# A four-layer graph network: single-head f1 rows and a fourth adjacency buffer in the decoder, later pair additions, a moved bias row, and a merged weight product cut in two

## The chip, the cores and the metric

The kernel runs on one core of a Trainium2 chip. The metric is the device time of one execution in microseconds (us), as the median of several runs. Beside the runs there is one profiled execution, from which every view of the profile comes.

## The reference

Everything is float32. There are 2708 nodes with 512 features, and one dense adjacency matrix of zeros and ones (about 1.2% ones, ones on the diagonal). Four layers follow each other, each with a residual and a layer norm: x = layernorm(x + layer(x, adj)).

Layer 0 is an attention encoder, an MLP, and a decoder that uses the same attention again. The adjacency is given to it twice (as "local" and as "long range" pattern), so that both halves of `att` are the same. It has 4 heads of 128 features:

```
Xw  = per head  x @ W                       f1, f2 = Xw . V[:,0], Xw . V[:,1]
att = softmax over j of sigmoid(f1[i] + f2[j]), where adj[i, j] is not 0
Xn  = batchnorm(att @ Xw)
emb = batchnorm(elu(Xn @ enc_W.T + b) + Xn)
Y   = elu(per head (att @ emb) @ W.T)
out = batchnorm(elu(Y @ dec_W.T + b) + Y)
```

Layer 1 is A @ (x W + b) with each row divided by the node's degree. Layer 2 is a masked softmax attention with scores (x E)(x E).T. Layer 3 is a softmax attention with query, key and value weights, to whose scores the adjacency is added twice:

```
attn = softmax((x Wq + bq) @ (x Wk + bk).T / sqrt(512) + adj + adj);   out = attn @ (x Wv + bv)
```

## The kernel before, in words

Nodes are cut into 22 blocks of 128 (the last has 20). The whole of layer 0 works on transposed tiles: rows of a tile are the neighbours j of one block, its columns the nodes i of one half (`HSPAN`: two halves of 1354). The four heads go in two pairs (`HP` = 2). An attention pass (`attention_pass`) has therefore four passes, (half, pair) = (0,0), (0,1), (1,0), (1,1), of 22 blocks each, in the order `ORDER`; a block's index in that order is its *place*. The function runs twice: as the encoder (`first` true) and as the decoder.

For each block `form` makes the tile `t` of both heads (128 x 2708): it loads the adjacency block `a` (677 KB) on the SP queue (L369), ScalarE takes a tanh of the row f1 plus the block's f2 for each head (L396), VectorE multiplies by the adjacency (L404, which turns what is not linked into a large negative number), and ScalarE takes the exponential of both heads (L405). TensorE then multiplies it into six accumulators `po` (L471). There are four buffers of `t`, and of `a` four in the encoder and three in the decoder. The rows f1, broadcast to all partitions, come as one tile `f1b` of both heads in two buffers (L423). Five of the 22 tiles of each pass are written to memory by the encoder (`KEPT`) and read back by the decoder instead of being formed. In the passes of the first pair the encoder also prepares the adjacency itself: VectorE makes a mask `z` (L385, a tag with one buffer), adds it (L386), and POOL writes the block to `adj_d` (L390), from which the later passes read. In the decoder VectorE also counts the zeros of each block for layer 1 (`count`, L346).

In the encoder TensorE also adds up the columns of each tile (`psm`, L494). In the passes of the second pair, places 4 to 19 are first added in pairs on VectorE (L488), in place in the first tile of the pair, so that TensorE sums one tile for two.

At the end of an encoder pass `keep` copies the accumulators into `ft` (L580), and after pass (0,1) it makes the product of the MLP's weights with the batch norm's beta (L585: `small_product`, whose result goes through one row, here a tile with the tag "z"). Sums go through memory (`sum_d`, `few`, `rs_d`, `rb`) and their reciprocals scale `ft` in steps that are taken up between the places of the next pass.

Between encoder and decoder wq and wk are transposed into `wqT` and `wkT`, the MLP's weights are scaled by the batch norm (L684, L688), the query and key weights of layer 3 are merged into one 512 x 512 matrix `mqk` (L696, four row blocks of four matmuls; L705 writes it to `mqk_d`), and the MLP runs over six chunks of columns (L724), with a second small product for the mean (L733). At the end of a decoder pass `take` moves the accumulators out (L825); after the last one comes the decoder's MLP (L859, `ps_dec`), whose statistics give the last batch norm. The hidden rows of layer 1 follow at once (`tp_out` L996, `ps_hid` L128 by L998); before them VectorE clears a part of `hid_hi` (L966) and copies the weights into `w_sb` (L976).

The order of the instructions on each engine is laid out when the kernel is compiled, by a scheduler that takes readiness into account; each engine then works in that order. A buffer of a pool is reused when the last reader of its former tile is done, and a pool that opens in the room of a closed one waits for the last users of that room, transfers included. `tc.issue_after(x)` keeps an instruction behind x.

The lines that hold the f1 rows and the pair additions:

```
f1b = att.tile([P, HP, HW], F32, tag="f1b", name="f1b", bufs=2)
...
whole, m = before, P
nc.vector.tensor_tensor(whole[:n, :, :w], whole[:n, :, :w], tv, ALU.add)
```

Of the kernel before, what the change touches and what calls it, by code (L numbers as in the profile page):

```python
# [1 line left out]

# [6 lines left out]
F32 = mybir.dt.float32  # L9
# [3 lines left out]
AF = mybir.ActivationFunctionType  # L13
ALU = mybir.AluOpType
# [3 lines left out]
P = 128  # L18
# [11 lines left out]
def gnn_stack_kernel(  # L30
# [25 lines left out]
    nc = tc.nc  # L56
    N, F = x.shape
    H = w0.shape[1]
    C = F // P
# [103 lines left out]
    dram = ctx.enter_context(tc.tile_pool(name="dram", bufs=1, space=bass.MemoryType.DRAM))  # L163
    adj_d = dram.tile([N, N], F32, name="adj_d")
    mqk_d = dram.tile([C, P, C, P], F32, name="mqk_d")
    qscale = float(1.0 / F**0.5)
    uq = const.tile([P, C], F32, name="uq")

# [2 lines left out]
    with ExitStack() as l0:  # L171
# [40 lines left out]
        def project(att, psum):  # L212
# [97 lines left out]
                    copies(f2h[:, NT - 1, :])  # L310
                    nc.vector.tensor_scalar(bm1, prm_sb[:, MB_DEC, :], 1.0, None, ALU.subtract)

            return f1b, blocks, spread, rest

        def spread_sums(att, hf, p):

# [15 lines left out]
        def attention_pass(values, first, att, psum, finish, f1b=None, blocks=(), spread=None, rest=None, taken={}):  # L332
# [5 lines left out]
            def count(hf, jt, att, a=None):  # L338

                h0, w = HSPAN[hf]  # L340
                j0, n = BLOCKS[jt]
                if a is None:
                    a = att.tile([P, HW], F32, tag="a", name="a", bufs=3)
                    nc.sync.dma_start(a[:n, :w], adj_d[j0 : j0 + n, h0 : h0 + w])
                z = att.tile([P, HW], U8, tag="z", name="z", bufs=1)
                nc.vector.tensor_scalar(  # L346
                    z[:n, :w],
                    a[:n, :w],
                    -0.5 * BIG,
                    None,  # L350
                    ALU.is_lt,
                    ALU.add,
                    accum_out=zeros[:n, jt, hf : hf + 1],
                )

            def form(hf, p, jt, att, prepare, f1b, tv):
# [4 lines left out]
                if prepare and hf == 0 and jt < len(blocks):  # L361
                    a = blocks[jt]
                else:
                    a = att.tile([P, HW], F32, tag="a", name="a", bufs=4 if first else 3)

                    early = prepare and hf == 0 and jt < len(blocks) + 2
                    with tc.issue_after(spread.ins) if early else nullcontext():
                        loads.append(
                            nc.sync.dma_start(a[:n, :w], src[j0 : j0 + n, h0 : h0 + w])  # L369
                        )  # L370
# [23 lines left out]
                for k in range(HP):  # L394
                    h = HP * p + k
                    nc.scalar.activation(  # L396
                        tv[:, k, :],
                        f1b[:n, k, :w],
                        AF.Tanh,
                        bias=f2h[:n, jt, h : h + 1],  # L400
                        scale=0.5,
                    )
# [13 lines left out]
            for hf, (h0, w) in enumerate(HSPAN):  # L416
                for p in range(H // HP):
                    prepare = first and p == 0
                    if f1b is None or not prepare or hf > 0:
                        f1b = att.tile([P, HP, HW], F32, tag="f1b", name="f1b", bufs=2)  # L420

                        with tc.issue_after(loads[-9].ins) if len(loads) > 8 else nullcontext():
                            nc.sync.dma_start(  # L423
                                f1b[:, :, :w],
                                f1_d[HP * p : HP * (p + 1), h0 : h0 + w].partition_broadcast(P),
                            )
                    rb = None if first else spread_sums(att, hf, p)
                    sums = None
                    if first and rest is None:
                        sums = sum_tiles()  # L430
                    before = None
                    for place, jt in enumerate(ORDER):
                        n = BLOCKS[jt][1]

# [24 lines left out]
                        if po is None:  # L459


                            both = [
                                psum.tile([P, HP, BANK], F32, tag=f"po{q}", name="po", bufs=1)
                                for q in range(HB)
                            ]
                            po = [both[q][:, k, :] for k in range(HP) for q in range(HB)]
                        for k in range(HP):
                            h = HP * p + k
                            for q, (q0, qw) in enumerate(HCH[hf]):
                                r = 0 if n == P else q * Q  # L470
                                nc.tensor.matmul(  # L471
                                    po[HB * k + q][:, :qw],
                                    values[r : r + n, jt, h * P : (h + 1) * P],
                                    t[r : r + n, k, q0 : q0 + qw],
                                    start=(place == 0),
                                    stop=(place == NT - 1),
                                )
                        if not first:
                            continue

                        if prepare or not ALONE <= place < NT - LAST:
                            whole, m = t, n
                        elif place % 2 == 0:
                            before = t
                            continue
                        else:
                            whole, m = before, P
                            nc.vector.tensor_tensor(  # L488
                                whole[:n, :, :w], whole[:n, :, :w], tv, ALU.add
                            )  # L490
                        for k in range(HP):
                            for r, (q0, qw) in enumerate(SCH[hf]):

                                nc.tensor.matmul(  # L494
                                    sums[k][32 * r : 32 * r + 32, :SW],
                                    ones32[:m],
                                    whole[:m, k, q0 + qw - SW : q0 + qw],
                                    start=(place == 0),
                                    stop=(place == NT - 1),
                                )  # L500
                    later += finish(hf, p, po, sums if first else rb) or []
            for work in later:
                work()
# [59 lines left out]
        with (  # L563
# [8 lines left out]
            def keep(hf, p, po, sums):  # L572
# [4 lines left out]
                for k in range(HP):  # L577
                    for q, (q0, qw) in enumerate(HCH[hf]):
# [1 line left out]
                        taken[q % 2] = copy(  # L580
                            ft[:, HP * p + k, h0 + q0 : h0 + q0 + qw], po[HB * k + q][:, :qw]
                        )
                if hf == 0 and p == 1:
                    row = att.tile([P, HW], F32, tag="z", name="row", bufs=1)[:1, :F]
                    ps = small_product(po[0], mlp_w[0], prm_sb[:, B_ENC, :], row)  # L585
                    nc.vector.tensor_tensor(bias[:, 0, :], ps, prm_sb[:, MB_ENC, :], ALU.add)
                sm = [att.tile([P, BW], F32, tag="rs", name="sm") for _ in range(HP)]
                if not final:
                    for k in range(HP):
# [50 lines left out]

            attention_pass(xw, True, att, psum, keep, f1b, blocks, spread, rest, taken)
            scale1, mean1 = batch_scale(stats, G_ENC, "bn1")


            emb = rows_tile("emb")
# [28 lines left out]
        with (  # L674
            tc.tile_pool(name="att_c", bufs=1) as att,
            tc.tile_pool(name="ps_c", bufs=1, space=PSUM) as psum,
        ):

            (enc_w,) = mlp_w
            for c in range(C):
                if c % 2:
                    nc.scalar.activation(  # L684
# [4 lines left out]
                        enc_w[:, c, :], enc_w[:, c, :], scale1[:, c : c + 1], None, ALU.mult  # L689
                    )  # L690
            stats = stats_tile("stats_b", NCH)
            mqk = emb[:, NT - 3 * C : NT - 2 * C, :]
            for c in range(C):
                ps = psum.tile([P, F], F32, tag="misc", name="ps_m", bufs=2)
                for o in range(C):
                    nc.tensor.matmul(  # L696
                        ps,
                        wqT[:, o, c * P : (c + 1) * P],
                        wkT[:, o, :],
                        start=(o == 0),  # L700
                        stop=(o == C - 1),
                    )
                nc.scalar.activation(mqk[:, c, :], ps, AF.Copy, scale=qscale)
            for o in range(C):
                nc.gpsimd.dma_start(mqk_d[o], mqk[:, :, o * P : (o + 1) * P])  # L705

            row = emb[:1, NT - 3 * C - 2 : NT - 3 * C, :]
            pu = small_product(
                psum.tile([P, F], F32, tag="misc", name="ps_u", bufs=2),
                wkT,  # L710
# [5 lines left out]
            for ci, (c0, w) in enumerate(CHUNKS):  # L716
                pss = []
                for o in range(C):
# [10 lines left out]
                            stop=(c == C - 1),  # L729
                        )  # L730
                    pss.append(ps)
                    if ci == 0 and o == 0:
                        pm = small_product(  # L733
                            psum.tile([P, F], F32, tag="misc", name="ps_mean", bufs=2),
                            enc_w,
                            mean1,
                            row[:, 1, :],
                        )
                        nc.vector.tensor_tensor(bias[:, 0, :], bias[:, 0, :], pm, ALU.subtract)
                        nc.vector.tensor_scalar(  # L740
                            bias[:, 1, :], bias[:, 0, :], 1.0, None, ALU.subtract
                        )
                for o in range(C):
                    dst = ft[:, o, c0 : c0 + w]
                    r = elu(
# [22 lines left out]
            dec_w = load_mlp(dec_wT, "dec_w")  # L768
            links = {}
            spare = []  # L770

            def centre(pm):

# [33 lines left out]
            def decode(hf, p, po, rb):  # L807
# [45 lines left out]
                def mlp(q, o, st, wide):  # L853
# [2 lines left out]
                    q0, qw = HCH[hf][q]  # L856
                    ps = psum.tile([P, BANK], F32, tag="misc", name="ps_dec", bufs=2)
                    for c in range(C):
                        nc.tensor.matmul(  # L859
                            ps[:, :qw],  # L860
                            dec_w[:, c, o * P : (o + 1) * P],
                            t[:, c, q0 : q0 + qw],
# [70 lines left out]
                for q in range(HB):  # L933
# [8 lines left out]
                    if q == 0:  # L942
                        centre(po[0])
                    mlp(q, 3, st, True)

            attention_pass(emb, False, att, psum, decode)
        dsum = small.tile([P, NT], F32, tag="dsum", name="dsum")
# [811 lines left out]
```

## Time and profile before

| what | value |
|---|---|
| median of 3 runs | 3288.74 us (3287.61 to 3291.08) |
| the profiled execution's own time | 3290.97 us |
| its span in the profile | 3289.2 us |
| mean granted TensorE clock | 0.991 |
| TensorE busy | 3221.7 us (98%) |
| VectorE, ScalarE busy | 1944.6 us (59%), 1348.5 us (41%) |
| encoder attention | about 45 to 574 us |
| weights, encoder MLP | about 574 to 703 us |
| decoder attention, its MLP | about 703 to 1202 us |
| layer 1 | about 1209 to 1515 us |
| layers 2 and 3 | about 1515 to 3289 us |

How to read the views: PE is TensorE (PEld its weight loads), DVE VectorE, ACT ScalarE, POOL GpSimd, SP the engine that issues most transfers. L471 is line 471 of the kernel before. A float32 matmul appears as two passes, so that 12 passes are six matmuls. A row of the timeline has start, length, engine, line, operation, what is written and read, and the number of instructions merged; the bracket at its end is the idle time of that engine before it, with the instruction that ended it. A row of the busy times by stretch has the stretch, its length, the busy time of PE, PEld, DVE, ACT and POOL with counts of instructions, the granted TensorE clock as a share of full speed, the busy share of the transfer engines, and GB/s.

### The profile page before, as it was taken

The page shows a single profiled execution, that of the slowest core. Times are in us where ns is not written, and L with a number is a line of the kernel's source. Part 1 is how long each engine was busy: PE and PEld are TensorE (multiplying, and loading weights), DVE is VectorE, ACT ScalarE, POOL GpSimd, SP SyncE. Part 2 cuts the span into 40 slices and gives each one's busy share as a digit, 9 for nine tenths or more (in the row PEclk, how much of TensorE's full clock was granted, in tenths as well). Part 3 has the DMA queues.
Part 4 walks back from the last instruction along what each step waited for, and adds up shares of the span by engine and source line. Part 5 has one row for each costly group of instructions (what it writes and reads, how often), then busy time and mean ns, then how long its engine had stood idle before and what let it go on. Part 6 is the DMA issues. An engine that isn't in the chain of part 4 may idle for free.

```text
span 3289.2 us, 30359 instructions
## 1 busy us (share of the span) xinstructions
PE 3221.7 (98%) x10922; PEld 1722.4 (52%) x10922; DVE 1944.6 (59%) x3144; ACT 1348.5 (41%) x1512; POOL 129.7 (4%) x211
## 2 busy tenths in 40 slices
PE   8998999999999999999999999999999999999999
PEld 5443444454444445885555555554455555555554
DVE  7877977767687596445136666777252452543433
ACT  6887887557877753001133434443020120210211
POOL 1100100000000000000011000000000000000000
PEclk9999999999999999999999999999999999999999
DMA  8855863335555322550034444554211111111100
GB/s 283 305 187 171 302 233 124 106 102 183 185 179 172 134 81 67 144 145 21 0 102 133 122 124 136 148 159 125 68 49 33 44 31 43 40 34 43 36 24 20
DMA packets 172550, 381.45 MB, mean 116 GB/s; under 512 B 20938, under 2 KB 115094, under 8 KB 167982
## 3 DMA queue, kind: packets, MB, share of 16 engines
q1 hardware_dynamic: 156926, 308.16, 30.9%
q0 software_dynamic: 15472, 71.33, 5.8%
q8 instruction: 86, 1.41, 0.2%
q14 instruction: 66, 0.54, 0.1%
HBM read 307.22 MB, written 71.67 MB: 115 GB/s over the span
## 4 chain that ended last, share of the span: by engine, by line
PE 88%; DVE 5%; ACT 2%; DMA 2%; issue 1%; SPq 0%; DVEq 0%; ACTq 0%
PE po L1324 23%; PE po L471 19%; PE ps_s L1203 18%; PE ps_nb L1056 6%; PE ps_wide L1105 4%; PE psm L494 3%; DVE t L404 2%; PE ps_hid L128 2%; PE ps_sup L1501 2%; PE ps_o L1432 2%; PE ps_mlp L724 2%; PE ps_dec L859 2%; DMA a<-adj_d 1%; ACT t L405 1%; ACT t L396 1%
## 5 line engine op out<-in xcount | busy, mean ns | idle before, releaser
L404 DVE SCALAR_TENSOR_TENSOR t<-t,a 128x2708 f32<-128x2708 f32 (+1 forms) x156 | 462.2, 2975 | 124.1 <-ACT t L396 120.1
L396 ACT ACTIVATE t<-f1b,f2h 128x1354 f32<-128x1354 f32 (+1 forms) x312 | 428.3, 1413 | 60.5 <-PE po L471 28.7
L471 PE MATMUL po<-t,xw 128*128 128x452 f32 (+3 forms) x1056 | 415.9, 557 | 14.6 <-ACT t L405 14.6
L405 ACT ACTIVATE t<-t 128x2708 f32<-128x2708 f32 (+1 forms) x156 | 382.6, 2455 | 112.7 <-DVE t L404 112.4
L471 PE MATMUL po<-t,emb 128*128 128x452 f32 (+3 forms) x1056 | 403.1, 550 | 12.3 <-ACT t L405 9.2
L1203 PE MATMUL ps_s<-sup,hT 128*128 128x384 f32 (+1 forms) x1176 | 407.4, 490 | 0.0
L1324 PE MATMUL po<-sup,e 128*128 128x512 f32 x882 | 407.0, 595 | 0.0
L1324 PE MATMUL po<-e,xs 128*128 128x384 f32 (+1 forms) x1176 | 406.0, 489 | 0.0
L1635 DVE SCALAR_TENSOR_TENSOR e<-a_cols,ps_s 128x384 f32<-128x384 f32 (+1 forms) x154 | 85.5, 556 | 451.1 <-PE ps_s L1203 428.2
L471 PEld LDWEIGHTS po<-t,xw 128*128 128x128 f32 (+1 forms) x1056 | 191.5, 193 | 227.4 <-issue 202.0
L1203 PEld LDWEIGHTS ps_s<-sup,hT 128*128 128x128 f32 x1176 | 221.8, 190 | 164.2 <-issue 14.2
L471 PEld LDWEIGHTS po<-t,emb 128*128 128x128 f32 (+1 forms) x1056 | 194.9, 192 | 213.5 <-issue 188.7
L1324 PEld LDWEIGHTS po<-e,xs 128*128 128x128 f32 x1176 | 222.2, 190 | 160.2 <-issue 5.8
L1324 PEld LDWEIGHTS po<-sup,e 128*128 128x128 f32 x882 | 160.4, 190 | 159.3 <-issue 137.1
L1203 PE MATMUL ps_s<-hT 128*128 128x384 f32 (+5 forms) x672 | 211.1, 461 | 0.9 <-ACT sup L1508 0.7
L1302 ACT ACTIVATE e<-e 128x384 f32<-128x384 f32 (+1 forms) x308 | 151.7, 522 | 116.0 <-DVE e L1301 113.3
L1056 PE MATMUL ps_nb<-hid_hi,at 128*128 128x512 f32 x484 | 185.4, 390 | 0.4 <-DVE at L1048 0.4
L1550 ACT ACTIVATE a_cols<-a_cols,neg_big 128x384 f32<-128x384 f32 (+1 forms) x154 | 94.7, 617 | 220.9 <-DMA a_cols<-in_adjT_dram 183.3
L1056 PE MATMUL ps_nb<-hid_lo,at 128*128 128x512 f32 x462 | 179.9, 389 | 0.0
L108 ACT ACTIVATE ln_rstd<-ln_rstd 128x1 f32<-128x1 f32 (+1 forms) x88 | 17.2, 201 | 391.7 <-DVE ln_rstd L107 391.2
L1301 DVE TENSOR_TENSOR e<-e,nmax 128x384 f32<-128x384 f32 (+1 forms) x308 | 163.1, 552 | 23.3 <-ACT nmax L1294 23.3
L1203 PEld LDWEIGHTS ps_s<-hT 128*128 128x128 f32 x672 | 123.1, 190 | 89.5 <-issue 19.4
(252 smaller groups left out, 3325.8 us busy)
## 6 DMA issues: line engine op xcount, KB each, us to landing
a<-adj_d SPq DMA_DIRECT2D x110, 677.0 KB
a_cols<-in_adjT_dram SPq DMA_DIRECT2D x378, 192.0 KB
a<-in_adjT_dram SPq DMA_DIRECT2D x42, 677.0 KB
adj_d<-a POOLq DMA_DIRECT2D x42, 677.0 KB, 5.5
raw<-in_adjT_dram SPq DMA_DIRECT2D x105, 256.0 KB
kept<-t POOLq DMA_DIRECT2D x16, 1354.0 KB, 6.8
t<-kept SPq DMA_DIRECT2D x16, 1354.0 KB
a_cols<-in_adjT_dram SPq DMA_DIRECT2D x63, 202.0 KB
```

The source lines that it names most:

```text
L396: nc.scalar.activation(tv[:, k, :], f1b[:n, k, :w], AF.Tanh, bias=f2h[:n, jt, h : h + 1], scale=0.5,)
L404: step = nc.vector.scalar_tensor_tensor(tv, tv, GUARD, ab, ALU.add, ALU.mult)
L405: nc.scalar.activation(tv, tv, AF.Exp, scale=0.5)
L471: nc.tensor.matmul(po[HB * k + q][:, :qw], values[r : r + n, jt, h * P : (h + 1) * P], t[r : r + n, k, q0 : q0 + qw], start=(place == 0), ...
L494: nc.tensor.matmul(sums[k][32 * r : 32 * r + 32, :SW], ones32[:m], whole[:m, k, q0 + qw - SW : q0 + qw], start=(place == 0), stop=(place = ...
L1056: nc.tensor.matmul(pos[it][:n], at, half[:, jt, :], start=(jt == 0 and k == 0), stop=(jt == NT - 1),)
L1105: nc.tensor.matmul(ps[:, :width], w(c, o), xt(c), start=(c == 0), stop=(c == C - 1),)
L1203: nc.tensor.matmul(ps[:, b * P : w], keys[:, c, j0 : j0 + P], st["q"][:, c, b * P :], start=(c == 0), stop=(c == C - 1),)
L1301: nc.vector.tensor_tensor(e, e, st["nmax"][:, :w], ALU.add)
L1302: nc.scalar.activation(e, e, AF.Exp)
L1324: nc.tensor.matmul(out, lhsT, rhs, start=(k == 0), stop=(k == NT - 1))
L1550: nc.scalar.activation(a, a, AF.Identity, bias=neg_big[: a.shape[0]], scale=1.0e30)
```

## The change

1. *Decoder, f1 rows.* In the decoder the row of each head is a tile of its own, in three buffers. The first head's row is loaded on the SP queue, the second head's on POOL's. The encoder keeps the tile of both heads.
2. *Decoder, adjacency.* `a` has four buffers there too.
3. *Encoder, pair additions.* The addition of a pair of tiles, and its column sums, are taken up at the next place: the addition is kept behind the next tile's multiplication by the adjacency, and the sums stand ahead of that tile's matmuls.
4. *Bias of the encoder's MLP.* The product with beta after pass (0,1) and the product with the mean are gone; one product with the shift (beta - mean x scale) is made from the unscaled weights, before they are scaled and before the MLP.
5. *Merged weights.* Two of the four row blocks of `mqk` stay where they were. `wkT` and half of `wqT` are written to memory from POOL, read back on SP into two `t` buffers at the end of the decoder, and the other two row blocks are made there, behind the last matmul of the decoder's MLP; ScalarE copies them out and POOL writes them to `mqk_d`.

The diff, cut to its core:

```
+    wqT_d = dram.tile([P, C, C // 2 * P], F32, name="wqT_d")
+    wkT_d = dram.tile([P, C, F], F32, name="wkT_d")
...
-                    a = att.tile([P, HW], F32, tag="a", name="a", bufs=4 if first else 3)
+                    a = att.tile([P, HW], F32, tag="a", name="a", bufs=4)
...
+                        else:
+                            f1b = [
+                                att.tile([P, HW], F32, tag="f1b", name="f1b", bufs=HP + 1)
+                                for k in range(HP)
+                            ]
+                            with early:
+                                nc.sync.dma_start(f1b[0][:, :w], f1[:, 0, :])
+                            nc.gpsimd.dma_start(f1b[1][:, :w], f1[:, 1, :])
...
+                        if waiting is not None:
+                            waiting(step)
+                            waiting = None
                         for k in range(HP):
...
+                        def add_up(whole, m, more, first_one, last_one, behind=None):
+                            if more is not None:
+                                with tc.issue_after(behind.ins):
+                                    nc.vector.tensor_tensor(
+                                        whole[: more.shape[0], :, :w],
+                                        whole[: more.shape[0], :, :w],
+                                        more,
+                                        ALU.add,
+                                    )
+                            for k in range(HP):
+                                for r, (q0, qw) in enumerate(SCH[hf]):
+                                    nc.tensor.matmul(
...
+                        if single:
+                            add_up(t, n, None, place == 0, place == NT - 1)
                         else:
+                            waiting = partial(add_up, before, P, tv, False, False)
...
-                if hf == 0 and p == 1:
-                    row = att.tile([P, HW], F32, tag="z", name="row", bufs=1)[:1, :F]
-                    ps = small_product(po[0], mlp_w[0], prm_sb[:, B_ENC, :], row)
-                    nc.vector.tensor_tensor(bias[:, 0, :], ps, prm_sb[:, MB_ENC, :], ALU.add)
...
+            shift1 = batch_shift(scale1, mean1, B_ENC, "bn1")
...
+            merged(0)
+            (enc_w,) = mlp_w
+            row = emb[:1, NT - 3 * C - 2 : NT - 3 * C, :]
+            pm = small_product(
+                psum.tile([P, F], F32, tag="misc", name="ps_shift", bufs=2),
+                enc_w,
+                shift1,
+                row[:, 1, :],
+            )
...
+            nc.gpsimd.dma_start(wkT_d, wkT)
+            nc.gpsimd.dma_start(wqT_d, wqT[:, :, half * P :])
+            merged(1)
             for o in range(C):
-                nc.gpsimd.dma_start(mqk_d[o], mqk[:, :, o * P : (o + 1) * P])
+                nc.gpsimd.dma_start(
+                    mqk_d[o][:, :half, :], mqk[:, :half, o * P : (o + 1) * P]
+                )
...
-                    if ci == 0 and o == 0:
-                        pm = small_product(
-                            psum.tile([P, F], F32, tag="misc", name="ps_mean", bufs=2),
...
+                nc.sync.dma_start(wk_again, wkT_d)
+                nc.sync.dma_start(wq_again, wqT_d)
+                with tc.issue_after(last_dec[0].ins):
+                    for c in range(half):
+                        for o in range(C):
+                            nc.tensor.matmul(
+                                po[1 + c],
+                                wq_again[:, o, c * P : (c + 1) * P],
+                                wk_again[:, o, :],
+                                start=(o == 0),
+                                stop=(o == C - 1),
+                            )
+                for c in range(half):
+                    nc.scalar.activation(mqk[:, c, :], po[1 + c], AF.Copy, scale=qscale)
+                    nc.gpsimd.dma_start(
+                        mqk_d[:, :, half + c, :].rearrange("o p i -> p o i"),
+                        mqk[:, c, :].rearrange("p (o i) -> p o i", o=C),
+                    )
```

## The prediction

> **What bounds the kernel now.** I read the page first: is one engine the bound, and does its clock hold?
>
> ```profile
> PE 3221.7 (98%) x10922; PEld 1722.4 (52%) x10922; DVE 1944.6 (59%) x3144; ACT 1348.5 (41%) x1512; POOL 129.7 (4%) x211
> PEclk9999999999999999999999999999999999999999
> ```
>
> TensorE is busy for 98% of the span. Only two things can pay: TensorE work taken away, and TensorE gaps. So next I read the busy times by stretch (length; then PE, PEld, DVE, ACT, POOL busy; clock; DMA share; GB/s).
>
> ```profile
> 225.00:300.00 75.00, 70.42 (x279) 31.22 (x281) 52.16 (x22) 61.97 (x39) 1.60 (x3) 0.95 0.45 151
> 300.00:330.00 30.00, 20.99 (x90) 8.80 (x83) 25.99 (x25) 17.05 (x11) 3.31 (x6) 0.83 0.63 207
> 482.00:574.00 92.00, 87.32 (x347) 38.90 (x336) 65.92 (x34) 71.30 (x44) 1.60 (x3) 0.96 0.41 141
> 590.00:705.00 115.00, 112.72 (x359) 55.11 (x358) 85.83 (x128) 53.11 (x67) 3.79 (x6) 1.00 0.25 87
> 705.00:800.00 95.00, 89.74 (x242) 43.59 (x240) 62.35 (x40) 76.51 (x47) 0.26 (x1) 1.00 0.52 177
> 800.00:912.00 112.00, 105.72 (x277) 51.87 (x278) 74.98 (x57) 88.58 (x57) 0.00 (x0) 0.97 0.54 181
> 1202.00:1216.00 14.00, 6.89 (x13) 3.29 (x14) 12.98 (x30) 11.28 (x19) 0.00 (x0) 0.63 0.52 179
> ```
>
> The gaps lie in layer 0. The timeline of TensorE names them (start, length, line, passes; in brackets the idle time before, and who ended it).
>
> ```profile
> 276.39 10.94 PE L471 MATMUL po<-t,xw 128*128 128x452 f32 x24 [2.69 <-ACT t L405]
> 300.49 3.59 PE L546 MATMUL po<-enc_w,prm_sb 128*1 128x512 f32 x8
> 304.86 1.05 PE L551 MATMUL po<-ones,row 1*128 1x1 f32 x8 [0.77 <-DVE row L549]
> 314.14 6.29 PE L471 MATMUL po<-t,xw 128*128 128x452 f32 x12 [8.24 <-ACT t L405]
> ...
> 586.20 13.97 PE L696 MATMUL ps_m<-emb 128*128 128x512 f32 x32 [0.91 <-DVE ft L638]
> ...
> 792.06 4.82 PE L471 MATMUL po<-t,emb 128*128 128x452 f32 x12 [1.24 <-ACT t L405]
> 802.57 7.81 PE L471 MATMUL po<-t,emb 128*128 128x452 f32 x12 [5.69 <-ACT t L405]
> 911.80 8.56 PE L471 MATMUL po<-t,emb 128*128 128x452 f32 x14 [3.03 <-DVE ot L825]
> 1209.11 0.48 PE L996 MATMUL tp_out<-ident,ot 128*128 128x128 f32 x1 [7.53 <-DVE ot L990]
> ```
>
> A gap costs twice: 12 passes last 4.82 us in the row at 792.06, 7.81 us after 5.69 us of idling.
>
> **Part by part.**
>
> *1. The bias row leaves the encoder's turn to its second half.* `keep` makes the product with B_ENC there and copies its row into tag "z", of which there is one buffer. VectorE shows what that holds up:
>
> ```profile
> 304.12 0.68 DVE L549 COPY row<-po 1x512 f32<-1x512 f32 x1 [2.70 <-PE po L546]
> 306.02 0.87 DVE L385 TENSOR_SCALAR z<-a 128x1354 f32<-128x1354 f32 x1
> ```
>
> The next pass must prepare adjacency through the same z. It cannot before 306.02, so its first tile reaches TensorE at 314.14. Lost from 300.49 on: 13.65 us, and 6.29 - 4.82 = 1.5 us of slow passes, 15.1 in all. In the changed order VectorE forms two tiles of the new pass before it copies po out; it idles 9 us there now. By its rows (0.87 + 1.57 + 2.97 a tile, 2.98 for place 21, from 285.8) both are multiplied by 298.6, and the copies slip 0.6 us. The third tile's exponential ends near 311.5, against a need at 300.5 + 2 x 6.03 = 312.6. **Gain 14.5** (9 to 15.1).
>
> *2. Pair additions behind the next tile.* In the compiled order most additions already stood there; the one of places 16 and 17 moves. Today it waits for TensorE with the next two tiles queued behind it: the 2.69 us before 276.39, and again in the second half. Moved, that tile's multiplication runs 268.2 to 271.1 and the addition to 274.0, so the sums, due at 272.35, start 1.7 us late instead. I take 1 us in each half: **gain 2** (-1 to 6).
>
> *3. The merged weights and the mean.* 32 passes take 13.97 us; 16 of them go from this stage, 7.0 us. The separate mean product (4.6 us) becomes the shift product, so it stays once; but it moves ahead of the MLP, and the bias is ready before the first ELU, so that the waits of 1.36 and 0.73 us at 607.5 and 624.3 go. Against this: the buffer of ps_m turns free only when ScalarE, queued behind the first tanh (594 to 595 us, when its rows land), has copied it; the shift row's copy is queued behind `linked`, which waits for rb; and 1.5 MB of weights for the end of the decoder are now written just then from POOL, ahead of head 1's first row on its queue, which delays that row and the first adjacency blocks by 3 to 4 us. That is 2 to 4 us of new standing. 9.1 less 3: **gain 6** (2 to 9).
>
> *4. Decoder: a fourth adjacency buffer.* VectorE waits 31.4 us there for adjacency, 15 times, and its z and product stand before the takes of po. Idle on TensorE: 0.46 + 0.43 + 1.24 + 5.69 + 0.68 + 3.03 + 0.20 + 0.46 = 12.2 us, and slow passes 3.0 (802.57) and 3.1 (8.56 against 14 x 0.379 + 0.17). A load takes 3.8 us from issue, and is issued when a product frees a buffer; with one more buffer it goes out one product earlier, 3 us or more. What is late next: ScalarE, at 5.0 us a formed tile against TensorE's 4.55; but 5 of 22 tiles of a pass are not formed, and four t buffers give a tile 13.7 us for its 8. I leave 1 us for each of four edges: **gain 14** (6 to 18).
>
> *5. f1 rows of single heads.* Head 0's row has the third buffer. Head 1's must wait for the last tanh of head 0, and POOL issues it. Behind the wait on POOL: nothing until the next row. In ScalarE's order 5.0 us of work follow (exp 2.4, two tanh), then the first tanh that needs the row. No row of this trace is this load; nearest is adj_d<-a from POOL, also 677 KB:
>
> ```profile
> adj_d<-a POOLq DMA_DIRECT2D x42, 677.0 KB, 5.5
> mqk_d<-emb POOLq DMA_DIRECT2D x4, 256.0 KB, 4.4
> out_dram<-sup POOLq DMA_DIRECT2D x18, 256.0 KB, 3.4
> ```
>
> So ScalarE stands about 1 us at each of three turns, before the exponential of place 21, which has 2.6 us to spare. **Cost 0.** One rule speaks against it: the Trainium skill, "SBUF — State Buffer", section "SBUF: two separate sides", says that POOL cannot write the descriptors of its DMA while VectorE holds the port they share. But 5.5 was measured with VectorE over 90% busy (106 of 116 us from 330 to 446), so the row has that in it; with a whole 2.98 us product added, 8.5, the exponential would still be in time. Both give 0 (-1 to 6).
>
> *6. The other half of the merged product at the end.* 16 passes, 7.0 us, fit the idle 7.53 us before 1209.11, and the weights come back long before. But the last write of mqk_d lies in memory that the next stage reuses: the clearing of hid_hi on VectorE now waits for it, and behind it stand the copy of w_sb and so every ps_hid. ScalarE takes the second half after four `ot` (1206.9 + 2.7), to 1210.2; POOL's 256 KB take 3.4 us (2.7 to 4.4), to 1213.7; clearing and copy 1.6. The first ps_hid starts at 1215.4, not 1209.4. SP's b_sb and first layer 1 adjacency wait for the write too, but are needed only from 1221 and 1297. The first two blocks then need 6.9 us and about 2.5 of slow clock, to 1224.8; now they end at 1219.8. **Loss 5** (0 to 9).
>
> The clock rule of the skill ("TensorE: Matmul & The Clock Gate", "Part 1: The HAM clock gate") weighs on parts 4 and 6: idling past a window of about 3.4 us halves the rate until TensorE was busy that long, so 1.7 us a gap, and none for the 3.03. Part 4 would then give 14 - 4.4 = 9.6 and the sum would be 28. The rows say 3.0 and 3.1, and 10.94 against 9.37 even after 2.69 us; I take the rows.
>
> Sum: 14.5 + 2 + 6 + 14 - 5 = **31.5 us**. Layers 1 to 3 have TensorE busy 1980 of 1992 us, untouched. The profiled execution took 3290.97 us (span 3289.2), 2.2 above the median of the runs, so it becomes 3259.5 and the median 3288.74 - 31.5 = 3257.
>
> **Rivals.**
> - *The buffer doesn't pay*: ScalarE (77 of 95 us busy) or DMA bandwidth, not the buffer count, sets the decoder. For it: one kept read on SP's queue can hold the loads behind it. Against: the waits name adjacency, at half the DMA share. Part 4 gives 3: 3268.
> - *The turn only half closes*, because the first tile's exponential or `few` comes late: part 1 gives 6, so 3266.
> - *The end is free*: the write lands unnoticed, part 3 keeps 8: gain 38.5, 3250.
> - *Slower*: head 1's row comes late. Its limit is about 8.6 us after issue; beyond it each us stands TensorE a us at three turns. To eat 31.5 and 6.6 more it must take 8.6 + 38/3 = 21 us: 3295. Slowest landing of the same size from POOL: 9.0.
>
> **How the numbers follow.** Main case 0.62, buffer 0.14, half turn 0.07, free end 0.14, late row 0.03. A measurement tells about 0.2%, 6.6 us, from no change; only the last case and mishaps together come near: faster 0.96, same 0.02, slower 0.02. The parts' bounds added as independent errors give 8 us to the better and 12 to the worse side; the range takes in the rivals but the last: 3244 to 3271.
>
> **What would show it.** Right: no ps row between psm near 300.5 and the next po; z before the last copies; 16 passes in ps_m; decoder gaps under 2 us, no wait of z for adjacency near a turn's end; ps_hid starting some 14 us after the end of the last ps_dec instead of 8. Wrong: a tanh with f1b late at each turn; gaps at places 5 to 10 ended by ScalarE; a first ps_hid held long past the mqk write.

## The result, and the profile after

The changed kernel takes **3284.11 us** (median, 3281.2 to 3286.79) against 3288.76 us of the kernel before in the same runs: ratio 0.9985, 95% interval 0.9979 to 0.9992. That is faster by 4.7 us, where 31.5 had been predicted. The profiled execution has a span of 3282.6 us, 6.6 less than before.

The page still shows one engine at 98%, and is no help by itself:

```profile
PE 3215.0 (98%) x10906; PEld 1722.1 (52%) x10906; DVE 1943.8 (59%) x3144; ACT 1347.6 (41%) x1512; POOL 135.3 (4%) x219
```

The busy times by stretch (columns as in the prediction) say where to look: 300 to 316 is the encoder's turn, 684 to 1029 are the first three decoder passes, 1187 to 1210 is the way into layer 1.

```profile
300.00:316.00 16.00, 16.00 (x80) 6.80 (x78) 14.78 (x11) 14.88 (x10) 3.00 (x5) 1.00 0.61 199
684.00:785.00 101.00, 91.94 (x244) 45.10 (x243) 64.03 (x43) 79.56 (x48) 1.33 (x3) 0.97 0.54 175
785.00:897.00 112.00, 104.25 (x276) 50.95 (x274) 75.91 (x56) 89.99 (x58) 0.55 (x1) 0.97 0.52 174
897.00:1029.00 132.00, 128.92 (x341) 64.12 (x342) 103.74 (x102) 91.42 (x64) 0.53 (x1) 0.98 0.46 158
1187.00:1210.00 23.00, 17.31 (x41) 7.87 (x40) 20.24 (x47) 19.88 (x34) 1.54 (x2) 0.85 0.37 119
```

The encoder's turn is full (16.00 of 16). The decoder lacks 9.1, 7.8 and 3.1 us. The timeline of TensorE after names those gaps; they are the rows that answer to 802.57 and 911.80 of before, a new one at 1028.67, and the start of layer 1:

```profile
784.48 7.06 PE L490 MATMUL po<-t,emb 128*128 128x452 f32 x12 [4.64 <-ACT t L409]
897.49 6.88 PE L490 MATMUL po<-t,emb 128*128 128x452 f32 x12 [6.47 <-ACT t L409]
1028.67 5.54 PE L490 MATMUL po<-t,emb 128*128 128x452 f32 x14 [2.59 <-DVE ot L858]
1198.48 1.09 PE L1061 MATMUL tp_out<-ident,ot 128*128 128x128 f32 x8 [1.74 <-ACT wq_again L1005]
1203.52 9.79 PE L129 MATMUL ps_hid<-w_sb,ot 128*128 128x512 f32 x16 [3.95 <-DVE w_sb L1041]
```

Over the whole decoder TensorE idles 21.7 us, against 12.2 before. Besides these turns, 1.87 and 2.55 us of it lie inside the first pass (before 734.35 and 755.36) and 1.76 us before 886.20, all ended by ScalarE.

The waits of the decoder (engine and line, what it waits for, us in total, times, longest), first of before, then of after:

```profile
DVE t L404 <- ACT t L396: 77.6, 25, 5.7
ACT t L405 <- DVE t L404: 71.3, 39, 5.8
DVE z L346 <- DMA a<-adj_d: 31.4, 15, 4.0
```

```profile
DVE t L408 <- ACT t L400: 88.8, 30, 5.4
ACT t L409 <- DVE t L408: 76.5, 42, 5.2
DVE z L350 <- DMA a<-adj_d: 32.1, 14, 5.6
```

The buffer that was to end the waits for adjacency left them at 32.1 us. VectorE and ScalarE wait longer for each other. The TensorE timelines of the profiled executions give the time of each stage, and with it the stage that failed (the decoder is its first `po` to the end of the last `ps_dec`; the stages meet at 586.2, 694.4, 1201.6 and 1297.5 us before):

| stage | before | after | change | predicted |
|---|---|---|---|---|
| encoder, to the first `ps_m` | 586.2 | 569.4 | -16.8 | -16.5 (parts 1, 2) |
| middle, to the first decoder `po` | 108.2 | 104.5 | -3.7 | -6 (part 3) |
| decoder | 507.2 | 516.0 | **+8.8** | **-14** (parts 4, 5) |
| to the first `ps_nb` | 95.9 | 100.9 | +5.0 | +5 (part 6) |

### The profile page after: what moved, and what is told of

It reads as the page before. It is cut to its first block, busy times and chain, and to the rows that moved or that the text cites. A ratio compares the mean times of both kernels' runs of the same rounds, so it can differ in the third digit from the quotient of the medians.

```text
span 3282.6 us, 30374 instructions
## 1 busy us (share of the span) xinstructions
PE 3215.0 (98%) x10906; PEld 1722.1 (52%) x10906; DVE 1943.8 (59%) x3144; ACT 1347.6 (41%) x1512; POOL 135.3 (4%) x219
## 4 chain that ended last, share of the span: by engine, by line
PE 79%; issue 9%; DVE 5%; ACT 4%; DMA 2%; POOL 0%; SPq 0%; DVEq 0%; ACTq 0%; POOLq 0%
PE po L1389 23%; PE ps_s L1268 17%; PE po L490 11%; PE ps_nb L1121 6%; PE ps_wide L1170 4%; PE ps_hid L129 2%; PE ps_sup L1566 2%; PE ps_o L1497 2%; ACT t L409 2%; ACT t L400 2%; DVE t L408 2%; PE ps_dec L892 2%; PE ps_mlp L767 2%; PE psm L519 1%; PE ps_s L1260 1%
## 5 line engine op out<-in xcount | busy, mean ns | idle before, releaser
L490 PE MATMUL po<-t,emb 128*128 128x452 f32 (+3 forms) x1056 | 402.6, 550 | 21.7 <-ACT t L409 19.1
```

Source lines behind the costliest of these rows:

```text
L490: nc.tensor.matmul(po[HB * k + q][:, :qw], values[r : r + n, jt, h * P : (h + 1) * P], t[r : r + n, k, q0 : q0 + qw], start=(place == 0), ...
```

## The experiments

Theory: the decoder's edit does harm through the order in which it lets the scheduler lay out VectorE and ScalarE. Rivals: the harm comes from the other parts; the buffer pays and single rows eat it; the decoder is bound by something that no adjacency buffer touches. All times are medians of four or five runs, and ratios are to the kernel before in the same session. Its median was 3286.6 to 3288.8 us in the sessions, so that differences between kernels of two sessions are good to some 2 us.

### Which part carries the loss

`dec_as_before` (in `enc_alone` the merged product also goes back to the middle as a whole; `three_a` sets only bufs=3; `dec_alone` is the kernel before with the opposite of this diff):

```
-  a = att.tile(..., tag="a", bufs=4)
+  a = att.tile(..., tag="a", bufs=4 if first else 3)
-  f1b = [att.tile([P, HW], F32, tag="f1b", bufs=HP + 1) for k in range(HP)]
+  both = att.tile([P, HP, HW], F32, tag="f1b", bufs=2)      # one DMA on SP
```

> The changed kernel with the decoder's buffers as they were (pair rows in two buffers, three of adjacency); all else stays. My theory: the decoder's 8.6 us of loss (shift of -20.5 us at its start, -11.9 at the end of its MLP) come from the decoder's own edit, which changes the order that the scheduler gives to ScalarE and VectorE and adds nothing, as the waits for adjacency (31.4 us before, 32.1 after) did not go. Then about 3275.5 us, and PE gaps of about 12 us in the decoder instead of 21.7. Rival: the loss comes with the earlier start, the weights written to memory at the decoder's start or the reshuffled order alone; then 3284 +- 2 and gaps near 20 us. Rival two: the fourth buffer does pay and is eaten elsewhere; then slower than 3288.

> The kernel before with the decoder's edit alone (single rows in three buffers, four of adjacency). My theory: slower than before by up to 9 us, 3289 to 3298; decoder gaps of some 20 us against 12.2. Rival (the loss is of the other parts): the predicted gain, up to 14 us, or none: 3275 to 3289.

> The changed kernel with three adjacency buffers in the decoder, single rows kept. If the fourth buffer is worth nothing (my theory): 3284 +- 3. If the single rows cost and the buffer pays, this is the worst of both: 3290 to 3298. If the buffer itself does the harm through the order it leads to: 3276.

> The changed kernel with the decoder's buffers as before and the merged product whole in the middle: what is left is the encoder (bias row, pair additions) and the shift product ahead of the MLP. If the parts add up as the profile's milestones say (encoder -16.8, end +0, middle at most -1): about 3271 us, faster than both. If the decoder loses whenever it starts earlier: 3278 to 3281.

| kernel | us | ratio to before, interval |
|---|---|---|
| dec_as_before | 3268.97 | 0.9941 (0.9927 to 0.9954) |
| dec_alone | 3304.97 | 1.0048 (1.0036 to 1.0061) |
| three_a | 3273.87 | 0.9957 (0.9944 to 0.9969) |
| enc_alone | 3271.25 | 0.9947 (0.9934 to 0.9959) |

The decoder's edit costs 15.1 us on top of the other parts (3284.11 - 3268.97) and 16.3 alone: more than the 9 that I expected, because it also costs 3.4 us in the middle stage (101.1 us in `dec_as_before`, 104.5 after). There the timeline of TensorE after, and one row of `dec_as_before`:

```profile
576.99 1.13 PE L711 MATMUL ps_m<-emb 128*128 128x512 f32 x2 [0.39 <-ACT emb L718]
579.56 1.05 PE L581 MATMUL ps_shift<-ones,emb 1*128 1x1 f32 x8 [1.44 <-DVE emb L579]
580.54 4.54 PE L711 MATMUL ps_m<-emb 128*128 128x512 f32 x6
```

```profile
578.70 1.05 PE L571 MATMUL ps_shift<-ones,emb 1*128 1x1 f32 x8 [0.20 <-DVE emb L569]
```

TensorE waits for two copies: that of `ps_m`, which ScalarE makes behind the first tanh (at 576.37, in `dec_as_before` ahead of it at 573.15), and that of the shift row, behind `linked` on VectorE. The six passes that follow then run at a granted clock of 0.63 (1.00 in `dec_as_before`).

Of the 15.1 us the fourth buffer makes 10.2 (after - `three_a`), the single rows 4.9 (`three_a` - `dec_as_before`). By the profiled executions 8.9 of the 10.2 lie in the decoder. 2.5 of the 4.9 are the middle stage's (103.6 us in `three_a`, with the same waits). Four buffers with pair rows were not run, so the split holds for this order of taking the parts away. The merged product cut in two is worth 2.3 us net.

One place of the harm can be read. VectorE after, ahead of the third turn, and the same place of `dec_as_before`:

```profile
1008.50 5.87 DVE L408 SCALAR_TENSOR_TENSOR t<-t,a 128x2708 f32<-128x2708 f32 x2 [3.92 <-ACT t L400]
1019.97 1.56 DVE L350 TENSOR_SCALAR_CACHE_REDUCE z<-a 128x1354 uint8<-128x1354 f32 x1 [5.61 <-DMA a<-adj_d]
1021.46 5.86 DVE L408 SCALAR_TENSOR_TENSOR t<-t,a 128x2708 f32<-128x2708 f32 x2
1027.24 3.65 DVE L858 SCALAR_TENSOR_TENSOR ot<-po,bn_scale,rb 128x452 f32<-128x452 f32 x6
```

```profile
1006.93 5.87 DVE L408 SCALAR_TENSOR_TENSOR t<-t,a 128x2708 f32<-128x2708 f32 x2 [4.62 <-ACT t L400]
1012.72 3.66 DVE L848 SCALAR_TENSOR_TENSOR ot<-po,bn_scale,rb 128x452 f32<-128x452 f32 x6
```

With four buffers a count z has been listed ahead of two products and of the takes of `po`. The block has not landed, VectorE stands for 5.61 us, and TensorE waits for the takes: the new 2.59 us before 1028.67. In the compiled order, 18, 24 and 38 full z (of blocks with 128 rows) stand ahead of the first, second and third takes before (and in `dec_as_before` and `three_a`), but 18, 26 and 39 after and in `dec_alone`. The gap that grew most, 6.47 us at the second turn, is ended by ScalarE; two more z stand ahead of the takes there, but no single wait of theirs was traced to it.

### Is it the place of z?

The diffs from here on show the core of each edit. In `z_behind_4a` (the changed kernel) and `z_behind_3a` (`dec_as_before`) z is held behind the block's own product; `no_z_4a` and `no_z_3a` leave out the counting. `z_behind_three_a` is `z_behind_4a` with three buffers.

```
-  if not first and p == (jt in KEPT[0]): count(hf, jt, att, a)
   ... tanh; step = product; exp
+  if not first and p == (jt in KEPT[0]):
+      with tc.issue_after(step.ins): count(hf, jt, att, a)
```

> The changed kernel, with the count of an adjacency block (z) kept behind the block's own product on VectorE. Theory: the scheduler, which sees a buffer free, puts z further ahead in VectorE's list; there it stands until the block has landed, with products that could run behind it, so that the fourth buffer moves the wait and does not take it away, and its list is worse. Then z finds its block long landed, the 32.1 us of waits of z for adjacency fall below 15, and the time is 3264 to 3274. Rival (ScalarE and VectorE take turns on four t buffers, and no order of z helps): 3281 to 3287.

> The same edit of z on the kernel with the decoder's buffers as before (pair rows, three of adjacency; 3269.0 us). Theory: z in its place takes away most of what the buffers were to take away: 3262 to 3269, and four buffers then differ from three by under 4 us. Rival: no effect or a loss, as the product holds its buffer 1.6 us longer: 3269 to 3275.

> The changed kernel without the count of zeros in the decoder: z is left out, and so are the adjacency blocks that are loaded only for it; the degrees of layer 1 are then wrong. Theory (z and its place carry the loss): 3258 to 3268, and within 4 us of the same edit on the decoder's old buffers. Rival (the fourth buffer or the single rows harm in another way): about 15 us slower than that kernel.

> The kernel with the decoder's buffers as before (3269.0 us), without the count of zeros in the decoder (left out as in the kernel no_z_4a). Theory: gaps of TensorE in the decoder go from 12.6 to under 5 us: 3258 to 3265. Rival (ScalarE bounds the turns, not z): 3267 to 3270.

> The kernel z_behind_4a (3272.43 us; single rows, z behind its product) with three adjacency buffers. If the fourth buffer's harm was the place of z alone, and the buffer itself is worth nothing: 3272 +- 2. If the buffer does help once z is in its place: 3275 to 3280. If it still harms: 3267 to 3270.

| | four buffers, single rows | three, single rows | three, pair rows |
|---|---|---|---|
| z as listed | 3284.11 | 3273.87 | 3268.97 |
| z behind its product | 3272.43 | 3269.64 | 3267.65 |
| no z | 3269.34 | not run | 3265.50 |

With z behind its product the changed kernel gains 11.7 us, and its gaps in the decoder fall from 21.7 to 14.1 us. The fourth buffer's harm falls from 10.2 to 2.8 us, which is no longer clear of noise: both kernels stand at 0.9949 of the kernel before, each in its own session. So most of the harm was the place of z. That z no longer waits for adjacency at all (no such row is left; in `z_behind_3a` one product waits 3.0 us) was expected; what came next was not. The gaps that the kernel before had stay. `z_behind_3a`, and `no_z_3a`, where nothing waits for adjacency:

```profile
774.27 6.18 PE L481 MATMUL po<-t,emb 128*128 128x452 f32 x12 [6.36 <-ACT t L407]
882.84 6.48 PE L481 MATMUL po<-t,emb 128*128 128x452 f32 x12 [4.94 <-DVE ot L849]
```

```profile
772.25 6.66 PE L476 MATMUL po<-t,emb 128*128 128x452 f32 x12 [5.65 <-ACT t L407]
881.29 6.75 PE L476 MATMUL po<-t,emb 128*128 128x452 f32 x12 [4.94 <-DVE ot L844]
```

The decoder's gaps on TensorE sum to 12.6 and 11.2 us in these two, against 12.2 before. So the 31 us of waits for adjacency were not what opened the turns; `no_z_3a` missed its forecast of under 5 us of gaps. VectorE of `no_z_3a` at the second turn shows what does:

```profile
875.78 2.98 DVE L406 SCALAR_TENSOR_TENSOR t<-t,a 128x2708 f32<-128x2708 f32 x1 [4.62 <-ACT t L398]
878.67 3.66 DVE L844 SCALAR_TENSOR_TENSOR ot<-po,bn_scale,rb 128x452 f32<-128x452 f32 x6
```

A product that waits 4.62 us for ScalarE stands before the takes.

### Is it the formation of tiles on ScalarE?

`short_act_4a` and `short_act_3a` shorten ScalarE's second pass over a tile; `kept_moved` changes places of `KEPT`:

```
-  nc.scalar.activation(tv, tv, AF.Exp, scale=0.5)
+  half = tv[:, :, : w // 2]; nc.scalar.activation(half, half, AF.Tanh, scale=0.5)   # decoder
-  step = nc.vector.scalar_tensor_tensor(tv, tv, GUARD, ab, ALU.add, ALU.mult)
+  step = nc.vector.scalar_tensor_tensor(tv, tv, GUARD, ab, ALU.add, ALU.is_lt)  # decoder
```

> The changed kernel in which the decoder's second ScalarE pass of a tile goes over half of its columns (a tanh in place of the exponential, and the mask is a comparison, so that values stay small; the attention weights are then wrong): 1.2 us less ScalarE work a tile, all else as in the changed kernel. Theory (ScalarE's formation is the bound): the gaps at the turns fall under 2 us, 3262 to 3270. Rival (adjacency or the takes are the bound): gaps stay, 3278 to 3284.

> The same shortened ScalarE pass on the kernel with the decoder's buffers as before (3269.0 us). Theory: gaps of TensorE in the decoder from 12.6 to under 5 us: 3258 to 3264, with the waits for adjacency still there (some 30 us), harmless. Rival (three adjacency buffers bound the turns): gaps stay or grow, 3267 to 3270.

> The kernel z_behind_3a (3267.65 us) with the kept tiles at other places: (2,6,11,16,20) and (1,7,11,15,19) in place of (4,8,11,14,18) and (3,7,11,15,19), so that at most four formed tiles stand in a row across a turn where there were six or seven. Theory: what opens the decoder's turns (6.36 and 4.94 us there, 5.65 and 4.94 even without any z) is ScalarE, at 5.05 us a formed tile against TensorE's 4.55, not adjacency. Then the two gaps fall to 1 to 2.5 us each and the time to 3257 to 3263. Rival (the takes of po behind a product of VectorE set the turn, wherever the kept tiles are): both gaps stay over 4 us, 3266 to 3270.

`short_act_3a` takes 3252.68 us, 16.3 less than `dec_as_before`. ScalarE is busy 69.08 us of the first pass instead of 85.52, and the gaps of the decoder sum to 2.2 us:

```profile
770.14 5.54 PE L481 MATMUL po<-t,emb 128*128 128x452 f32 x14 [0.60 <-DVE ot L849]
873.59 5.54 PE L481 MATMUL po<-t,emb 128*128 128x452 f32 x14 [1.23 <-DVE ot L849]
1000.42 5.54 PE L481 MATMUL po<-t,emb 128*128 128x452 f32 x14 [0.35 <-DVE ot L849]
```

ScalarE's time is not all that changed. The waits of z for adjacency, which I expected to stay at some 30 us (30.3 in `dec_as_before`), fall to 7.6, and the scheduler puts 25 and 39 z ahead of the second and third takes. The products ahead of the takes are the same (19, 36 and 53). But `no_z_3a` has no such waits at all and keeps its gaps, and more z ahead of the takes can only delay them. So the chain of tanh, product and exponential bounds the turns, with ScalarE as its longest part (two tanh and an exponential take some 5 us a tile, the product 2.97). `short_act_4a` takes 3266.28 us: two gaps of 3.77 us stay, both ended by the takes, which have one more product ahead of them (20 and 54 instead of 19 and 53). It stays 13.6 us behind `short_act_3a`: relief of ScalarE does not clean VectorE's list.

`kept_moved` missed: 3277.43 us, 9.8 slower than `z_behind_3a`. Its first `ps_m` comes 5.3 us later, and a gap opens inside the first decoder pass, while the turns keep 3.90, 4.95 and 3.83 us:

```profile
730.83 47.74 PE L481 MATMUL po<-t,emb 128*128 128x452 f32 x120 [4.84 <-ACT t L407]
```

It moved work without taking any away. Why the encoder lost was not settled. So four kernels keep more tiles instead. They form one or two tiles a pass less (`six_kept` and `seven_kept` on `z_behind_3a`, `six_kept_only` on `dec_as_before`, `six_kept_after` on the changed kernel):

```
-  KEPT = [(4, 8, 11, 14, 18), (3, 7, 11, 15, 19)]
+  KEPT = [(4, 8, 11, 14, 18, 21), (3, 7, 11, 15, 17, 20)]             # six
+  KEPT = [(4, 8, 11, 14, 16, 18, 21), (3, 7, 9, 11, 15, 17, 20)]      # seven
```

> The kernel z_behind_3a (3267.65 us) with six kept tiles a pass instead of five: places (4,8,11,14,18,21) and (3,7,11,15,17,20). ScalarE forms 16 tiles a pass instead of 17, 5 us less a pass. If ScalarE's formation bounds the decoder (short_act_3a gained 16.3 us for some 20 us of ScalarE work a pass less), about a quarter of that comes back: 3262 to 3266. Rival: the encoder pays for the extra writes, or the reads wait for a t buffer on SP with adjacency behind them, as may have cost kept_moved its 9.8 us: 3268 to 3277.

> The kernel six_kept (3259.7 us) with seven kept tiles a pass: places (4,8,11,14,16,18,21) and (3,7,9,11,15,17,20). If ScalarE still bounds the two turns left (3.57 and 4.08 us), another 2 to 5 us: 3255 to 3258. If the reads, each twice the bytes of the adjacency block that it saves, or the takes now set the turns: 3259 to 3265.

> The kernel dec_as_before (3269.0 us; z where the scheduler puts it) with six kept tiles a pass as in six_kept. If ScalarE is the bound and the place of z is worth little with three buffers (it was 1.3 us): 3260 to 3263. If six_kept owes its gain to z: 3266 to 3269.

> The changed kernel (3284.1 us) with six kept tiles a pass. If the fourth buffer's and the single rows' harm lies in VectorE's list, relief of ScalarE gives the same 8 us and leaves the difference of about 15 to six_kept_only: 3274 to 3278. If the harm comes from ScalarE being late: 3262 to 3266.

| kernel | us | against its base | gaps in the decoder |
|---|---|---|---|
| six_kept | 3259.68 | -8.0 | 8.1 |
| seven_kept | 3254.26 | -13.4 | 4.5 |
| six_kept_only | 3268.53 | -0.4 | 13.9 |
| six_kept_after | 3271.12 | -13.0 | 12.6 |

Real relief of ScalarE pays where z has its place. It pays nothing in `six_kept_only`, where the list moved a z forward (25 stand ahead of the second takes, 24 in its base), the waits of z for adjacency are 25.9 us, and the second turn's gap grew from 3.25 us:

```profile
885.75 7.42 PE L480 MATMUL po<-t,emb 128*128 128x452 f32 x12 [6.32 <-ACT t L409]
```

`six_kept` differs from it only in that z is held behind its product, and is 8.9 us faster. That ties the two causes together: late tiles open the turns, and, as I read it, a z ahead of its time makes tiles later.

`six_kept_after` gains most of the three with six tiles, and is left 2.6 us behind `six_kept_only`, so the forecast that 15 us would stay between these two was wrong. But `six_kept_only` carries a z moved forward itself; behind `six_kept` the loss is still 11.4 us. Whether the harm needs a late ScalarE to show stays open.

`seven_kept` is the fastest of the kernels that leave nothing out (`short_act_3a` leaves out half of the exponential): ratio to before 0.9897, interval 0.9884 to 0.9911. One long gap is left in its decoder:

```profile
875.21 7.83 PE L481 MATMUL po<-t,emb 128*128 128x452 f32 x12 [4.02 <-ACT t L407]
```

### Two smaller questions

`three_a_rows_sp` puts the second head's row on SP; `memset_pool` clears `hid_hi` on POOL:

```
-  nc.gpsimd.dma_start(f1b[1][:, :w], f1[:, 1, :])
+  nc.sync.dma_start(f1b[1][:, :w], f1[:, 1, :])
-  nc.vector.memset(hid_hi[:, NT - 1, :].bitcast(F32), 0.0)
+  nc.gpsimd.memset(hid_hi[:, NT - 1, :].bitcast(F32), 0.0)
```

> The kernel three_a (single rows, three adjacency buffers, 3273.9 us) with the second head's row issued on SP right after the first's, not on POOL. Two theories of what the single rows cost (4.9 us against pair rows): if it is the queue or the late landing of POOL's row, 3269 to 3271; if it is that the row has no free buffer until the last tanh of head 0 is done, SP now stands in that wait with adjacency loads behind it: 3274 to 3284.

> The kernel z_behind_3a (3267.65 us) with the clearing of hid_hi on POOL instead of VectorE. Theory of step 6: the clearing waits for the last write of mqk_d and holds the copy of w_sb behind it on VectorE, and so the first ps_hid (3.9 us of idle TensorE before it). Then the first ps_hid starts 2 to 4 us earlier: 3264 to 3266. Rival: w_sb lies in memory that waits for the same write: no change, 3267 to 3269.

`three_a_rows_sp` takes 3271.07 us (3270.28 to 3272.02), 2.8 less than `three_a`; the intervals of the two ratios overlap (0.9935 to 0.9962, 0.9944 to 0.9969), so a part of the single rows' 4.9 us may lie on POOL's queue, no more. A late row it is not: ScalarE waited for a row once after, 0.4 us, and 1.0 us in `three_a`.

`memset_pool` takes 3266.30 us, 1.3 less than its base with overlapping ranges, and the first `ps_hid` still comes 13.4 us after the last `ps_dec` (13.6 in the base). POOL's clearing is released by the write, and VectorE's copy starts with it:

```profile
1185.01 0.52 POOL L1022 MEMSET hid_hi<- 128x512 f32 x1 [2.14 <-DMA mqk_d<-wq_again]
1185.10 1.51 DVE L1032 COPY w_sb<-xs 128x2048 f32<-128x2048 f32 x1
```

In the compiled program the copy waits for the same POOL writes itself. The rival was right: the room of `w_sb` is what waits.

## Why the prediction was wrong

- **Parts 1 and 2, right as a sum.** 16.8 us against 16.5; the turn is full. The kernels with the old decoder show it too (16.8, and 17.5 in `enc_alone`). No run parts the two. In part 1 the rows as quoted put the second tile's multiplication at 299.6, not 298.6; nothing came of that, as the turn is full.
- **Part 3, right, but for the decoder.** 7.1 us in `dec_as_before` against 6; after it is 3.7, as the single rows put the two copies later. They are two of the waits that part 3 named, for `ps_m`'s copy behind the first tanh and the shift row's behind `linked`. That POOL's writes of the weights delay rows was not tested.
- **Part 4, wrong in sign: -10.2 instead of +14.** This is the step that failed. It read 31.4 us of waits for adjacency and gaps at the same turns as cause and effect. `z_behind_3a` and `no_z_3a` take the waits away (3.0 us and none) and the gaps stay (12.6, 11.2 us); `short_act_3a` takes ScalarE's time away and they go (2.2). The sentence "5 of 22 tiles of a pass are not formed, and four t buffers give a tile 13.7 us for its 8" argued ScalarE away by an average over the pass. The other error was to let the load move forward and leave the order as it was. More room moved z, not the end of the wait: 26 and 39 counts stood ahead of the second and third takes instead of 24 and 38, and holding z back gave 11.7 us.
- **Part 5, cost 0: measured 4.9**, within its range (-1 to 6). The row was in time, as said, at the three turns; 2.5 us of the cost lie in the middle stage, and the rest stays open.
- **Part 6, right in size:** 5.0 us against 5, and 13.7 us from the end of the last `ps_dec` to `ps_hid` against some 14. Its reason was half wrong: not only the clearing of `hid_hi` waits, the copy of `w_sb` does too.
- **The rival "the buffer doesn't pay"** named the right engine, but kept a gain of 3 us, for 3268. That `dec_as_before` came out at 3269 is no proof of it, as it has no fourth buffer. No rival let the buffer harm by the order it leads to.

The account: part 4 missed by 24.2 us and part 5 by 4.9; the rest came out at 19.7 (3288.64 - 3268.97) instead of 17.5, 2.2 better. That makes 26.9 of the 27.1 us by which 3284.1 missed 3257.

## What to carry to other kernels

A wait that stands near a gap is a cause only if the gap goes when the wait goes: ask which chain would end last without it, at that very place of the pass and not on its average. Where a scheduler lays out in-order lists, a free buffer is also leave to list early work earlier, ahead of what is urgent; count in the compiled order what stands before the takes (here 26 counts instead of 24) before a buffer is priced as a gain. The count is a warning and no price: `short_act_3a` had 25 and 39 and hardly a gap. Hold work that nothing waits for behind work that something waits for; then relief of the engine that is late can pay.

## What the runs showed of the hardware

- The same gap has no fixed price in slow passes. After 6.36 or 6.37 us of idling at the same turn, 12 passes took 6.18 us in `z_behind_3a`, 7.74 in `memset_pool` and 7.77 in `z_behind_three_a`; a row of 12 at full speed is 4.82 (792.06 of before). After 0.60 us, 14 passes took 5.54. The prediction's 3.0 us a gap is the upper end of 1.4 to 3.0 at this turn.
- A short gap can bring slow passes too. In the middle stage after, waits of 0.39 and 1.44 us stood ahead of six passes at a granted clock of 0.63 (580.5 to 585.1 us; `three_a` 0.67 behind 0.34 and 1.66 us); with 0.20 us in `dec_as_before` the clock stayed at 1.00.
- At the three turns the 677 KB row from POOL landed 4.3 to 5.1 us after its issue after, and 4.2 to 5.7 us in `three_a`. The one issued at 1010.1 us landed after 4.4, though VectorE was busy with two products from 1008.50 to 1014.37; a hold-up of POOL by a busy VectorE, the fear of part 5, did not show there. The first row of the decoder, at 568.8 us beside other loads (DMA share 0.98), took 7.0 us.
